# Five changes to a four-layer adjacency kernel: weight sums on VectorE, one eviction split over two engines, an own last turn, statistics ahead, 19 buffers for the residual

## Chip, cores, metric

One core of a Trainium2 chip. The metric is the time of one execution in microseconds (us), lower is better. Times below are medians. A ratio is the mean time of one kernel's fast runs over the mean time of the other's in the same rounds, so it is not quite the ratio of the two medians quoted.

## The reference

x has 128 graphs of 128 nodes with 256 features, float32. Four residual layers follow each other, each behind a layer norm and a relu. The last has two batch norms over all 128 x 128 rows, so nothing after either of them can start before every graph is through.

```python
h = relu(layernorm(x));  x = x + gnn(h, adj)        # layer 0: gates and a 128x128 matrix for each graph
h = relu(layernorm(x));  x = x + attention(h, adj)  # layer 1: causal, added bias
h = relu(layernorm(x));  x = x + slconv3(h, adj)    # layer 2: 256 -> 512 -> 1024 -> 256, mixed by adj*adj
h = relu(layernorm(x))                              # layer 3:
z = A_hat @ h @ W1.T + b1                           #   256 -> 512
o = relu(batchnorm(z)) @ W2.T + b2                  #   512 -> 256
out = x + batchnorm(o)
```

## The kernel before

Four graphs make a group g of T = 512 columns; there are 32 groups. Generators for the layers of several groups are stepped in an order written as a string: FILL for the filling of the pipeline, TURN for each turn after it. A large product is put together from products of quarters of its operands, seven of them in place of eight (`seven`), which needs sums of quarters of each weight (`seven_of`, once) and of each activation (`sums`). Names that begin with p are tiles in PSUM and stand for the products that write them: pc of layer 0, pt, pp and py of layer 1, pu_x near the start of layer 2 and pr at its end, pg and pz of layer 3's first half, po of its second; pm occurs in layers 0 and 2.

```python
    def seven_of(b, name, extra=None):
        ...                                            # four sums for each weight, once
        nc.gpsimd.tensor_tensor(t1, b12, b11, ALU.subtract)
        nc.gpsimd.tensor_tensor(t2, b22, t1, ALU.subtract)
        nc.gpsimd.tensor_tensor(t4n, b21, t2, ALU.subtract)
        nc.gpsimd.tensor_tensor(b12, b22, b12, ALU.subtract)

    def mixed(dst, src, aT, name, evict):
        for c in range(src.shape[-1] // P):
            pm = bank([P, G, P], f"{name}_{c}")
            for b in range(G):
                nc.tensor.matmul(pm[:, b, :], src[:, b, c * P : (c + 1) * P], aT, start=True, stop=True)
            evict(dst[:, c, :], pm.rearrange("p b n -> p (b n)"))
    ...
        h = norm(g, 2)                                 # in layer1(g)
        yield
        mT = w.tile([P, DC, T], FP, tag="dT", name=f"mT_{g}", bufs=2)
        mixed(mT, h, a2T, f"pm2_{g}", nc.scalar.copy)  # "mixed h": pu_x reads mT
    ...
    FILL = "apaapaaaaBBABBBBBBBpBABBBApBABBpABBpABBABB"
    ...
        for k in TURN:
            next(stream[k], None)
    ...
    EARLY, LATE = 4, 11                                # buffers for the residual x3 of the last stage
    ...                                                # pass two: z -> o, group by group; then
    for g in range(EARLY, EARLY + LATE):
        load_later(g)                                  # on GpSimd's queue
    sc2, sh2 = bn_affine(stats2, DC, g2_c, be2_c, "bn2", b2_c)
    ...                                                # scale o, transpose, add x3, store
```

Of the kernel before, what the change touches and what calls it, by code (L numbers as in the profile page):

```python
# [8 lines left out]
FP = mybir.dt.float32  # L9
AF = mybir.ActivationFunctionType  # L10
ALU = mybir.AluOpType
# [4 lines left out]
P = 128  # L16
LN_EPS = 1e-5
BN_EPS = 1e-5
# [4 lines left out]
def kernel(  # L23
# [39 lines left out]
    nc = tc.nc  # L63
    B, N, D = x.shape
    G = 4
    NG = B // G
    T = G * N
    DC = D // P
# [5 lines left out]
    FC = F1 // P  # L74
# [16 lines left out]

    zs = ExitStack()
    zp = zs.enter_context(tc.tile_pool(name="zp", bufs=2, side="right"))
    ZT = {}
# [17 lines left out]
    gw = weights.tile([P, 3, D], FP, name="gw")  # L112
    gb = const.tile([P, 3], FP, name="gb")
    nhalf = const.tile([P, 8], FP, name="nhalf")
    adjT = const.tile([P, P], FP, name="adjT")
    ain = const.tile([P, P], FP, name="ain")
    aout = const.tile([P, P], FP, name="aout")
    maskb = const.tile([P, P], FP, name="maskb")
    a2T = const.tile([P, P], FP, name="a2T")
    ahT = const.tile([P, P], FP, name="ahT")  # L120
    m_qk = weights.tile([P, DC, D], FP, name="m_qk")
# [3 lines left out]
    vecs = const.tile([P, NV], FP, name="vecs")  # L125
    stats1 = const.tile([P, FC, NG, 6], FP, name="stats1")
    stats2 = const.tile([P, DC, NG, 6], FP, name="stats2")
# [50 lines left out]
    for v in (b1, g1, be1, b2, g2, be2):  # L178
        k = v.shape[0] // P
# [18 lines left out]
    def seven_of(b, name, extra=None):  # L198


        b11, b21, b12, b22 = quarters(b)
        if extra is None:
            extra = weights.tile([P, 3, b.shape[1] // 2, b.shape[2] // 2], FP, name=f"{name}_s")
        operands = set_of(b, extra)
        t4n, t1, t2 = operands[3:6]
        nc.gpsimd.tensor_tensor(t1, b12, b11, ALU.subtract)
        nc.gpsimd.tensor_tensor(t2, b22, t1, ALU.subtract)
        nc.gpsimd.tensor_tensor(t4n, b21, t2, ALU.subtract)
        nc.gpsimd.tensor_tensor(b12, b22, b12, ALU.subtract)
        return operands  # L210
# [89 lines left out]
    LAST = NG - 1  # L300
# [25 lines left out]

    def mixed(dst, src, aT, name, evict):

        for c in range(src.shape[-1] // P):
            pm = bank([P, G, P], f"{name}_{c}")  # L330
            for b in range(G):
                nc.tensor.matmul(  # L332
                    pm[:, b, :], src[:, b, c * P : (c + 1) * P], aT, start=True, stop=True
                )
            evict(dst[:, c, :], pm.rearrange("p b n -> p (b n)"))

# [139 lines left out]
    def layer1(g):  # L476
# [83 lines left out]
        mT = w.tile([P, DC, T], FP, tag="dT", name=f"mT_{g}", bufs=2)  # L560
        mixed(mT, h, a2T, f"pm2_{g}", nc.scalar.copy)
        ex = w.tile([P, 3, 1, T // 2], FP, tag="ex", name=f"ms_{g}", bufs=2)
# [16 lines left out]
        uT = w.tile([P, HC1, T], FP, tag="uT", name=f"uT_{g}", bufs=1)  # L579
        mixed(uT, u, a2T, f"pmu_{g}", nc.vector.tensor_copy)  # L580
        ex = w.tile([P, 3, HC1 // 2, T // 2], FP, tag="us", name=f"us_{g}", bufs=1)
# [61 lines left out]
    def layer3(g):  # L643
# [3 lines left out]
        gT = w.tile([P, DC, T], FP, tag="dT", name=f"gT_{g}", bufs=2)  # L647
        mixed(gT, h, ahT, f"pg_{g}", nc.vector.tensor_copy)
        ex = w.tile([P, 3, 1, T // 2], FP, tag="ex", name=f"gs_{g}", bufs=2)
# [19 lines left out]
        yield from seven(columns_by_half(gs, SETS["b"], 0), put, [P, 2, T // 2], f"pz_{g}")  # L669




    TURN = "CCCBCCABBDABBCABBDDCBADCDDBDCCDBACBCCABCCACbBCBBCBCBBCBCBCdB"
    US = {}
    AHEAD = 3
# [5 lines left out]

    FILL = "apaapaaaaBBABBBBBBBpBABBBApBABBpABBpABBABB"
    stream = {"a": layer0(0), "p": prepare(), "B": layer1(0), "A": part(layer0, 1)}
# [5 lines left out]
    for g in range(NG):  # L690
        if g + AHEAD < NG:
            load_x(g + AHEAD)
        stream = {
            "A": part(layer0, g + 2), "B": bs, "C": layer2(g), "D": ds,
            "b": part(layer1, g + 2), "d": layer3(g),
        }
        for k in TURN:
            next(stream[k], None)
        assert all(next(stream[k], k) == k for k in "ABCD")
        bs, ds = stream["b"], stream["d"]  # L700
    for _ in ds:
        pass
    passA.close()

    def bn_affine(stats, nch, gam, bet, name, bias=None):


        mv = const.tile([P, nch, 2], FP, name=f"mv_{name}")
        for j in range(nch):
            nc.vector.bn_aggr(mv[:, j, :], stats[:, j].rearrange("p g s -> p (g s)"))  # L710
        mean = mv[:, :, 0]
        if bias is not None:
            mean = const.tile([P, nch], FP, name=f"mean_{name}")
            nc.vector.tensor_tensor(mean, mv[:, :, 0], bias, ALU.add)
        sc = const.tile([P, nch], FP, name=f"sc_{name}")
        inv_sqrt(sc, mv[:, :, 1], BN_EPS)
        nc.vector.tensor_tensor(sc, sc, gam, ALU.mult)
        sh = const.tile([P, nch], FP, name=f"sh_{name}")
        nc.vector.tensor_tensor(sh, mean, sc, ALU.mult)
        nc.vector.tensor_tensor(sh, bet, sh, ALU.subtract)  # L720
        if bias is not None:
            part = const.tile([P, nch], FP, name=f"part_{name}")
            nc.vector.tensor_tensor(part, bias, sc, ALU.mult)
            nc.vector.tensor_tensor(sh, sh, part, ALU.add)
        return sc, sh
# [4 lines left out]
    O = [keep.tile([P, DC, T], FP, name=f"o_{g}") for g in range(NG)]  # L730
    EARLY, LATE = 4, 11
    x3p = ctx.enter_context(tc.tile_pool(name="x3p", bufs=EARLY, reuse_waits="tile"))
# [3 lines left out]
    zw = zs.enter_context(tc.tile_pool(name="zw", bufs=2, side="right", reuse_waits="tile"))  # L736
    bw2T = keep.tile([P, FC, D], FP, name="bw2T")
    nc.scalar.dma_start(bw2T, BW2T)
    bw2s = keep.tile([P, 3, FC // 2, D // 2], FP, name="bw2s_late")
    nc.scalar.dma_start(bw2s, BW2S)  # L740
# [3 lines left out]
    R = {}  # L744
# [5 lines left out]

    def load_x3(g, pool, tag):
        R[g] = pool.tile([P, G, D], FP, tag=tag, name=f"x3i_{g}")
        nc.gpsimd.dma_start(R[g], X3[g])

    def second(g):
# [28 lines left out]
        def put(ij, pb, other):  # L784
# [7 lines left out]
            if done.count(j) == 2:  # L792
                nc.vector.bn_stats(stats2[:, j, g, :], O[g][:, j, :])

        yield from seven(product, put, [P, T // 2], f"po_{g}", zw)

    for n in range(1, 1 + AT_ONCE):
        load_z(n)
    sc1, sh1 = bn_affine(stats1, FC, g1_c, be1_c, "bn1", b1_c)
    PREPARE = FC + 1  # L800
# [3 lines left out]
    for n, g in enumerate(ORDER):  # L804
        then = second(ORDER[n + 1]) if n + 1 < NG else iter(())
        for _ in range(PREPARE):
            next(now)
            next(then, None)
# [12 lines left out]

    def load_later(g):
        load_x3(g, *((x3p, "x3") if g % (EARLY + LATE) < EARLY else (late, "x3l")))

    for g in range(EARLY, EARLY + LATE):
        load_later(g)
    sc2, sh2 = bn_affine(stats2, DC, g2_c, be2_c, "bn2", b2_c)
    for g in range(NG):
# [54 lines left out]
```

## Time and profile before

| | before |
|---|---|
| median of the three runs known before the prediction | 2664.24 us (2663.99 to 2666.74) |
| TensorE busy | 95% |
| one steady turn (from pr of a group to pr of the next) | 71.65 us |
| TensorE idle in the first 100 us | 50 us |
| gap between the two passes (wait for zo) | 8.0 us |
| from the last product of pass two to the end | 80.8 us |

TensorE is the engine to watch: read this way, a change gains only what it takes from TensorE's idle time, from its slow clock, or from the last stage, where DMA is full. The page's lines are in the prediction below.

### The profile page before, as it was taken

To read this page: it belongs to the slowest core of one execution; us is meant where nothing else is said; L and a number is where in the kernel's file an instruction comes from. 1 tells how busy PE (TensorE), PEld (TensorE's weight loads), DVE (VectorE), ACT (ScalarE), POOL (GpSimd) and SP (SyncE) were. 2 spreads that over 40 slices of the span, in tenths; PEclk is the share of its full clock that TensorE was granted. 3 is DMA by queue.
4 is the path that set the end of the run, shared out by engine and by line. 5 is a ranking of instruction groups with operands and counts; after the bars stand their busy time and mean duration, and the time that the engine had idled before them with its cause. 6 is when DMAs were issued, how large, how long until landed. Compare 5 with 4: busy or idle time off the path is not lost.

```text
span 2665.5 us, 40593 instructions
## 1 busy us (share of the span) xinstructions
PE 2541.2 (95%) x15215; PEld 2283.0 (86%) x15215; DVE 1904.5 (71%) x4743; ACT 1298.8 (49%) x2607; POOL 317.0 (12%) x616
## 2 busy tenths in 40 slices
PE   3899999999999999999999999999999999979984
PEld 2799999989998898999999899988989999968873
DVE  7677777777777777777777777777777776557775
ACT  3454444444455444454444444544454543336655
POOL 4111111111011110111111111111101111000011
PEclk7899999999999999999999999999999999989998
DMA  3000000000000000000000000000000000034469
GB/s 129 15 33 24 25 33 33 33 32 25 25 33 32 32 33 33 33 25 24 32 33 32 32 25 27 29 33 32 32 33 33 28 13 25 32 112 170 171 209 362
DMA packets 62055, 143.05 MB, mean 54 GB/s; under 512 B 4626, under 2 KB 39972, under 8 KB 57892
## 3 DMA queue, kind: packets, MB, share of 16 engines
q1 hardware_dynamic: 51636, 105.60, 11.1%
q0 software_dynamic: 9216, 33.56, 3.2%
q8 instruction: 120, 1.97, 0.3%
q10 hardware_dynamic: 1008, 1.31, 0.2%
q14 instruction: 75, 0.61, 0.1%
HBM read 73.48 MB, written 66.98 MB: 53 GB/s over the span
## 4 chain that ended last, share of the span: by engine, by line
PE 81%; DVE 6%; ACT 4%; DMA 4%; POOL 3%; issue 1%; ACTq 0%; POOLq 0%; DVEq 0%; SPq 0%
PE p_x L377 15%; PE p_z L377 8%; PE p_x L360 7%; PE pu_x L360 4%; PE pmu L332 4%; PE pz_x L377 4%; PE p_y L377 4%; PE po_x L775 3%; PE p_z L360 2%; ACT h L322 2%; PE pg L332 2%; PE pm L469 2%; PE py L551 2%; PE pqv_x L501 2%; PE pqv_x L496 2%; PE ps L521 2%
## 5 line engine op out<-in xcount | busy, mean ns | idle before, releaser
L322 ACT ACTIVATE h<-x,sh,rs 128x256 f32<-128x256 f32 x512 | 268.6, 589 | 386.4 <-POOL sh L319 386.4
L377 PE MATMUL p_x<-uT,w 128*128 128x256 f32 x1024 | 242.1, 379 | 0.0
L608 ACT ACTIVATE h2T<-h2T 128x512 f32<-128x512 f32 x192 | 120.4, 627 | 230.2 <-DVE h2T L607 230.2
L377 PEld LDWEIGHTS p_x<-uT,w 128*128 128x128 f32 x1024 | 189.6, 190 | 23.1
L315 POOL TENSOR_SCALAR rs<-mv 128x4 f32<-128x4 f32 x128 | 29.7, 232 | 1386.9 <-ACT h2T L608 1025.7
L311 DVE BATCH_NORM_STATS2 st<-x 128x6 f32<-128x256 f32 x512 | 190.4, 414 | 4.3 <-DMA x<-in_x_dram 2.1
L429 DVE SCALAR_TENSOR_TENSOR gs<-h,gw 128x256 f32<-128x256 f32 x384 | 163.3, 425 | 34.8 <-ACT h L322 28.8
L392 ACT COPY p_t<-p_x 128x512 f32<-128x512 f32 (+1 forms) x192 | 96.7, 504 | 114.6 <-PE p_x L377 101.9
L316 POOL TENSOR_TENSOR rs<-rs,nhalf 128x4 f32<-128x4 f32 x128 | 147.7, 1154 | 0.0
L332 PEld LDWEIGHTS pmu<-a2T,u 128*128 128x128 f32 x1024 | 119.5, 192 | 17.1 <-PE pr L636 7.4
L360 PEld LDWEIGHTS p_x<-w,h2T 128*128 128x128 f32 x1024 | 124.3, 192 | 3.3
L360 PE MATMUL p_x<-w,h2T 128*128 128x128 f32 x1024 | 124.6, 275 | 0.0
L574 ACT ACTIVATE u<-u 128x512 f32<-128x512 f32 x96 | 60.4, 631 | 131.8 <-DVE u L573 131.8
L764 ACT ACTIVATE zi<-zi,sh_bn,sc_bn 128x512 f32<-128x512 f32 x124 | 97.4, 812 | 55.4 <-DMA zi<-z 35.5
L332 PE MATMUL pmu<-a2T,u 128*128 128x128 f32 x1024 | 119.8, 275 | 1.8 <-ACT u L574 1.8
L377 PE MATMUL p_x<-us,w_s 128*128 128x256 f32 x512 | 121.3, 379 | 0.0
L377 PE MATMUL p_z<-us,w 128*128 128x256 f32 x512 | 121.2, 379 | 0.0
L377 PE MATMUL p_x<-uT,w_s 128*128 128x256 f32 x512 | 121.0, 379 | 0.0
L377 PE MATMUL p_y<-uT,w 128*128 128x256 f32 x512 | 121.0, 379 | 0.0
L377 PE MATMUL p_z<-us,w_s 128*128 128x256 f32 x512 | 121.0, 379 | 0.0
L377 PEld LDWEIGHTS p_z<-us,w 128*128 128x128 f32 x512 | 97.2, 190 | 13.5 <-ACT p_t L392 0.3
L377 PEld LDWEIGHTS p_z<-us,w_s 128*128 128x128 f32 x512 | 97.3, 190 | 13.2
(282 smaller groups left out, 6140.8 us busy)
## 6 DMA issues: line engine op xcount, KB each, us to landing
z<-zo SPq DMA_DIRECT2D x62, 512.0 KB, 2.6
zi<-z SPq DMA_DIRECT2D x31, 1024.0 KB, 4.8
x<-in_x_dram SPq DMA_DIRECT2D x32, 512.0 KB, 3.9
x<-x POOLq DMA_DIRECT2D x32, 512.0 KB, 3.0
x3i<-x POOLq DMA_DIRECT2D x32, 512.0 KB, 6.6
out_dram<-x3i SPq DMA_DIRECT2D x64, 256.0 KB, 8.3
w<-in_L_gnn_W_dram SPq DMA_DIRECT2D x1, 2048.0 KB
w<-in_L_gnn_W_dram SPq DMA_DIRECT2D x1, 1024.0 KB
```

The source lines that it names most:

```text
L311: nc.vector.bn_stats(st[:, b, :], xt[:, b, :])
L316: nc.gpsimd.tensor_tensor(rs, rs, nhalf[:, :G], ALU.pow)
L322: nc.scalar.activation(h[:, b, :], xt[:, b, :], AF.Relu, bias=sh[:, b : b + 1], scale=rs[:, b : b + 1])
L332: nc.tensor.matmul(pm[:, b, :], src[:, b, c * P : (c + 1) * P], aT, start=True, stop=True)
L360: nc.tensor.matmul(pb[:, rr, :], a_r[r][:, c, rr * P : (rr + 1) * P], b_r[r][:, c, :wide], start=(first and rr == 0 and c == 0), stop=(c = ...
L377: nc.tensor.matmul(pb[:, jj, :], b_r[r][:, c, at : at + P], a_r[r][:, c, :], start=(first and jj == 0 and c == 0), stop=(c == nk - 1), ski ...
L392: nc.scalar.copy(t, pb)
L429: nc.vector.scalar_tensor_tensor(gs, h[:, b, :], 1.0, gw[:, i, :], ALU.mult, ALU.mult, accum_out=gl[:, b, i : i + 1],)
L574: nc.scalar.activation(dst, dst, AF.Relu)
L608: nc.scalar.activation(dst, dst, AF.Relu)
L764: nc.scalar.activation(z, z, AF.Relu, bias=sh1[:, j : j + 1], scale=sc1[:, j : j + 1],)
L775: nc.tensor.matmul(pb, BW2R[r][:, c, :], a_r[r][:, c, :], start=(first and c == 0), stop=(c == FC // 2 - 1), skip_group_check=True,)
```

## The change

Its intent: take the port conflict between GpSimd and VectorE out of the filling, take the one wait of a steady turn away, cover the norm of the last group with products of the group before it, take 31 of 32 groups out of the statistics that have to wait for the last one, and load more of the residual ahead.

```diff
     (seven_of)
-        nc.gpsimd.tensor_tensor(t1, b12, b11, ALU.subtract)
+        nc.vector.tensor_tensor(t1, b12, b11, ALU.subtract)
     ... (the three other sums alike)
-            evict(dst[:, c, :], pm.rearrange("p b n -> p (b n)"))
+            evicts[c % len(evicts)](dst[:, c, :], pm.rearrange("p b n -> p (b n)"))
-        mixed(mT, h, a2T, f"pm2_{g}", nc.scalar.copy)
+        mixed(mT, h, a2T, f"pm2_{g}", (nc.vector.tensor_copy, nc.scalar.copy))
+    FINAL = "CCCCCCCCCCCCCCCCCCDCCDCCDdDDdDddDdDdddd"
-    FILL = "apaapaaaaBBABBBBBBBpBABBBApBABBpABBpABBABB"
+    FILL = "paaapaaaAaBBBBBABBBBBBBppABBAApBBABBBpBBAB"
-        for k in TURN:
+        for k in TURN if g < LAST else FINAL:
+    most1 = bn_part(stats1, FC, slice(LAST), "most1")      # 31 groups; joined with the last one later
     ... (bn_affine joins the two parts with six small operations)
-    EARLY, LATE = 4, 11
+    EARLY, LATE = 5, 14
-    bw2T = keep.tile([P, FC, D], FP, name="bw2T")
+    bw2T = second_w.tile([P, FC, D], FP, name="bw2T")      # freed after pass two
     for g in range(EARLY, EARLY + LATE):
-        load_later(g)
+        load_later(g, nc.sync)
     ... (small tiles move to pools that are freed earlier)
```

More of the change, by code (lines that the diff above doesn't have):

```diff
@@ L92 @@
     zs = ExitStack()
+    first = zs.enter_context(tc.tile_pool(name="first", bufs=1, side="right"))
     zp = zs.enter_context(tc.tile_pool(name="zp", bufs=2, side="right"))
@@ L112 @@
     gw = weights.tile([P, 3, D], FP, name="gw")
-    gb = const.tile([P, 3], FP, name="gb")
+    gb = weights.tile([P, 3], FP, name="gb")
     nhalf = const.tile([P, 8], FP, name="nhalf")
-    adjT = const.tile([P, P], FP, name="adjT")
-    ain = const.tile([P, P], FP, name="ain")
-    aout = const.tile([P, P], FP, name="aout")
-    maskb = const.tile([P, P], FP, name="maskb")
-    a2T = const.tile([P, P], FP, name="a2T")
-    ahT = const.tile([P, P], FP, name="ahT")
+    adjT = weights.tile([P, P], FP, name="adjT")
+    ain = weights.tile([P, P], FP, name="ain")
+    aout = weights.tile([P, P], FP, name="aout")
+    maskb = weights.tile([P, P], FP, name="maskb")
+    a2T = weights.tile([P, P], FP, name="a2T")
+    ahT = weights.tile([P, P], FP, name="ahT")
     m_qk = weights.tile([P, DC, D], FP, name="m_qk")
@@ L125 @@
     vecs = const.tile([P, NV], FP, name="vecs")
-    stats1 = const.tile([P, FC, NG, 6], FP, name="stats1")
+    stats1 = first.tile([P, FC, NG, 6], FP, name="stats1")
     stats2 = const.tile([P, DC, NG, 6], FP, name="stats2")
@@ L205, in seven_of @@
         t4n, t1, t2 = operands[3:6]
-        nc.gpsimd.tensor_tensor(t1, b12, b11, ALU.subtract)
-        nc.gpsimd.tensor_tensor(t2, b22, t1, ALU.subtract)
-        nc.gpsimd.tensor_tensor(t4n, b21, t2, ALU.subtract)
-        nc.gpsimd.tensor_tensor(b12, b22, b12, ALU.subtract)
+        nc.vector.tensor_tensor(t1, b12, b11, ALU.subtract)
+        nc.vector.tensor_tensor(t2, b22, t1, ALU.subtract)
+        nc.vector.tensor_tensor(t4n, b21, t2, ALU.subtract)
+        nc.vector.tensor_tensor(b12, b22, b12, ALU.subtract)
         return operands
@@ L325, in norm, with mixed @@
         return h
-    def mixed(dst, src, aT, name, evict):
+    def mixed(dst, src, aT, name, evicts):
         for c in range(src.shape[-1] // P):
@@ L579, in layer1 @@
         uT = w.tile([P, HC1, T], FP, tag="uT", name=f"uT_{g}", bufs=1)
-        mixed(uT, u, a2T, f"pmu_{g}", nc.vector.tensor_copy)
+        mixed(uT, u, a2T, f"pmu_{g}", (nc.vector.tensor_copy,))
         ex = w.tile([P, 3, HC1 // 2, T // 2], FP, tag="us", name=f"us_{g}", bufs=1)
@@ L647, in layer3 @@
         gT = w.tile([P, DC, T], FP, tag="dT", name=f"gT_{g}", bufs=2)
-        mixed(gT, h, ahT, f"pg_{g}", nc.vector.tensor_copy)
+        mixed(gT, h, ahT, f"pg_{g}", (nc.vector.tensor_copy,))
         ex = w.tile([P, 3, 1, T // 2], FP, tag="ex", name=f"gs_{g}", bufs=2)
@@ L669, in layer3, with bn_part @@
         yield from seven(columns_by_half(gs, SETS["b"], 0), put, [P, 2, T // 2], f"pz_{g}")
+    def bn_part(stats, nch, groups, name):
+        mv = const.tile([P, nch, 2], FP, name=f"mv_{name}")
+        for j in range(nch):
+            nc.vector.bn_aggr(mv[:, j, :], stats[:, j, groups].rearrange("p g s -> p (g s)"))
+        return mv[:, :, 0], mv[:, :, 1]
     TURN = "CCCBCCABBDABBCABBDDCBADCDDBDCCDBACBCCABCCACbBCBBCBCBBCBCBCdB"
+    FINAL = "CCCCCCCCCCCCCCCCCCDCCDCCDdDDdDddDdDdddd"
     US = {}
@@ L703, with bn_affine @@
     passA.close()
-    def bn_affine(stats, nch, gam, bet, name, bias=None):
-        mv = const.tile([P, nch, 2], FP, name=f"mv_{name}")
-        for j in range(nch):
-            nc.vector.bn_aggr(mv[:, j, :], stats[:, j].rearrange("p g s -> p (g s)"))
-        mean = mv[:, :, 0]
-        if bias is not None:
-            mean = const.tile([P, nch], FP, name=f"mean_{name}")
-            nc.vector.tensor_tensor(mean, mv[:, :, 0], bias, ALU.add)
+    def bn_affine(most, last, nch, gam, bet, name, bias):
+        (mean, var), (mean1, var1) = most, last
+        share = 1.0 / NG
+        d = const.tile([P, nch], FP, name=f"d_{name}")
+        nc.vector.tensor_tensor(d, mean1, mean, ALU.subtract)
+        nc.vector.scalar_tensor_tensor(mean, d, share, mean, ALU.mult, ALU.add)
+        nc.vector.tensor_tensor(mean, mean, bias, ALU.add)
+        nc.vector.scalar_tensor_tensor(d, d, share * (1.0 - share), d, ALU.mult, ALU.mult)
+        nc.vector.scalar_tensor_tensor(d, var, 1.0 - share, d, ALU.mult, ALU.add)
+        nc.vector.scalar_tensor_tensor(var, var1, share, d, ALU.mult, ALU.add)
         sc = const.tile([P, nch], FP, name=f"sc_{name}")
-        inv_sqrt(sc, mv[:, :, 1], BN_EPS)
+        inv_sqrt(sc, var, BN_EPS)
         nc.vector.tensor_tensor(sc, sc, gam, ALU.mult)
@@ L720, in bn_affine @@
         nc.vector.tensor_tensor(sh, bet, sh, ALU.subtract)
-        if bias is not None:
-            part = const.tile([P, nch], FP, name=f"part_{name}")
-            nc.vector.tensor_tensor(part, bias, sc, ALU.mult)
-            nc.vector.tensor_tensor(sh, sh, part, ALU.add)
+        part = const.tile([P, nch], FP, name=f"part_{name}")
+        nc.vector.tensor_tensor(part, bias, sc, ALU.mult)
+        nc.vector.tensor_tensor(sh, sh, part, ALU.add)
         return sc, sh
@@ L736 @@
     zw = zs.enter_context(tc.tile_pool(name="zw", bufs=2, side="right", reuse_waits="tile"))
-    bw2T = keep.tile([P, FC, D], FP, name="bw2T")
+    second_w = zs.enter_context(
+        tc.tile_pool(name="second_w", bufs=1, side="right", reuse_waits="tile")
+    )
+    bw2T = second_w.tile([P, FC, D], FP, name="bw2T")
     nc.scalar.dma_start(bw2T, BW2T)
-    bw2s = keep.tile([P, 3, FC // 2, D // 2], FP, name="bw2s_late")
+    bw2s = second_w.tile([P, 3, FC // 2, D // 2], FP, name="bw2s_late")
     nc.scalar.dma_start(bw2s, BW2S)
@@ L749, in load_z, with load_x3 @@
         ZT[ORDER[n]] = [z[:, :FC // 2, :], z[:, FC // 2 :, :]]
-    def load_x3(g, pool, tag):
+    def load_x3(g, pool, tag, queue=nc.gpsimd):
         R[g] = pool.tile([P, G, D], FP, tag=tag, name=f"x3i_{g}")
-        nc.gpsimd.dma_start(R[g], X3[g])
+        queue.dma_start(R[g], X3[g])
     def second(g):
@@ L792, in put @@
             if done.count(j) == 2:
-                nc.vector.bn_stats(stats2[:, j, g, :], O[g][:, j, :])
+                nc.vector.bn_stats(stats2[:, j, (g + 1) % NG, :], O[g][:, j, :])
         yield from seven(product, put, [P, T // 2], f"po_{g}", zw)
@@ L798 @@
         load_z(n)
-    sc1, sh1 = bn_affine(stats1, FC, g1_c, be1_c, "bn1", b1_c)
+    last1 = bn_part(stats1, FC, slice(LAST, NG), "last1")
+    sc1, sh1 = bn_affine(most1, last1, FC, g1_c, be1_c, "bn1", b1_c)
     PREPARE = FC + 1
@@ L805 @@
         then = second(ORDER[n + 1]) if n + 1 < NG else iter(())
+        if n + 1 == NG:
+            most2 = bn_part(stats2, DC, slice(LAST), "most2")
         for _ in range(PREPARE):
@@ L820, with load_later @@
     late = ctx.enter_context(tc.tile_pool(name="late", bufs=LATE, reuse_waits="tile"))
-    def load_later(g):
-        load_x3(g, *((x3p, "x3") if g % (EARLY + LATE) < EARLY else (late, "x3l")))
+    def load_later(g, queue=nc.gpsimd):
+        load_x3(g, *((x3p, "x3") if g % (EARLY + LATE) < EARLY else (late, "x3l")), queue)
     for g in range(EARLY, EARLY + LATE):
-        load_later(g)
-    sc2, sh2 = bn_affine(stats2, DC, g2_c, be2_c, "bn2", b2_c)
+        load_later(g, nc.sync)
+    last2 = bn_part(stats2, DC, slice(LAST, NG), "last2")
+    sc2, sh2 = bn_affine(most2, last2, DC, g2_c, be2_c, "bn2", b2_c)
     for g in range(NG):
```

## The prediction

> **What bounds the kernel now.** I read the page's head, then the table of engine time by stretches of the span, then the list of TensorE's waits, then the timeline around each wait. Each `profile` fence copies such lines.
>
> ```profile
> PE 2541.2 (95%) x15215; PEld 2283.0 (86%) x15215; DVE 1904.5 (71%) x4743; ACT 1298.8 (49%) x2607; POOL 317.0 (12%) x616
> ...
> 0.00:20.00 20.00, 6.99 (x29) 5.56 (x29) 10.86 (x44) 7.36 (x15) 7.97 (x21) 1.00 0.89 295
> 20.00:40.00 20.00, 1.87 (x4) 0.72 (x4) 18.96 (x20) 3.35 (x10) 17.74 (x14) 0.53 0.42 135
> 300.00:1300.00 1000.00, 991.38 (x6112) 902.53 (x6110) 731.55 (x1903) 487.53 (x992) 118.42 (x238) 1.00 0.08 30
> 2340.00:2360.00 20.00, 15.12 (x114) 13.41 (x113) 7.10 (x17) 3.04 (x8) 2.31 (x5) 0.98 0.22 79
> 2360.00:2380.00 20.00, 11.36 (x44) 9.13 (x44) 11.84 (x24) 3.98 (x8) 3.31 (x5) 0.76 0.54 203
> 2620.00:2640.00 20.00, 14.49 (x90) 10.49 (x88) 11.44 (x18) 14.72 (x21) 3.69 (x7) 0.91 1.06 396
> ```
>
> The columns of a stretch are its length, the busy time of TensorE, its weight loads, VectorE, ScalarE and GpSimd, then TensorE's clock, the DMA share and GB/s. TensorE bounds all but four places. The first 100 us hold about 50 us of its work. The steady turns leave 0.86% idle. The end of the first pass (2340 to 2380) leaves 13.5 us idle. From about 2576 to the end the DMA engines are full. No change of TensorE's work is in the diff, so the gain can only come out of these places.
>
> ```profile
> PE pu_x L360 <- ACT mT L335: 17.9, 29, 0.6
> PE pc L462 <- DVE m L452: 17.7, 4, 7.3
> PE po_x L775 <- ACT zo L764: 8.0, 1, 8.0
> PE pg L332 <- ACT h L322: 4.4, 1, 4.4
> ...
> 24.21 2.52 POOL L206 TENSOR_TENSOR w_s<-w 128x1024 f32<-128x1024 f32 x1
> 24.45 2.43 DVE L449 SCALAR_TENSOR_TENSOR m<-aout,gt,m 128x128 f32<-128x128 f32 x1
> 1358.61 2.07 ACT L322 ACTIVATE h<-x,sh,rs 128x256 f32<-128x256 f32 x4 [2.74 <-POOL sh L319]
> 1360.59 1.04 ACT L335 COPY mT<-pm 128x512 f32<-128x512 f32 x2
> 1361.21 1.13 PE L360 MATMUL pu_x<-w,mT 128*128 128x256 f32 x4 [0.62 <-ACT mT L335]
> 2359.86 3.78 PE L332 MATMUL pg<-ahT,h 128*128 128x128 f32 x16 [4.41 <-ACT h L322]
> 2575.51 0.54 POOL L753 DMA_DIRECT2D x3i<-x  x1 [195.64 <-PE po_x L775]
> ```
>
> The first four lines are the waits that the change aims at: total us, times, longest. Then the timeline shows a 128x128 VectorE operation of 2.43 us beside a weight sum on GpSimd; the steady wait; the wait at the end of the first pass with the slow matmuls after it; and the first late residual load.
>
> **What the Trainium skill says.** "SBUF — State Buffer", section "SBUF: two separate sides": VectorE with two SBUF inputs and GpSimd hold one port pair by an exclusive lock, and the loser blocks for a whole instruction. The trace agrees: m L449 takes 0.35 us with GpSimd quiet (at 63.43), 2.43 us above. "PSUM — Partial Sum Buffer", section "Specifications (TRN2)": ScalarE and VectorE read PSUM in parallel in different banks. The trace agrees: in the two evictions of hT the ScalarE copy starts at 1385.71 (0.59 us) and VectorE's at 1386.05 (0.69 us), neither stretched. "TensorE: Matmul & The Clock Gate", section "What's actually happening": an idle window of about 3.4 us halves the clock. Agrees: after 4.41 us idle the sixteen pg matmuls take 3.37 us in the chain, against 1.79 in steady turns. "DMA: Bandwidth & Descriptors", section "Issuing engines are not separate DMA queues": all queues run on the same 16 engines, and another queue saves only issue time. I use this for the last part; the before trace alone does not test it.
>
> **Part 1, weight sums on VectorE, new filling order.** Before, gl is ready at 21.7 us, and the twelve VectorE operations that build m run from 22.5 to 39.4, because the sums of w2 and w3 stand between them: a stretch of four GpSimd sums of 2.4 and four of 1.3 us. After, GpSimd is out of the way. VectorE pays for the sums: until gl it has twelve gate products at 0.47 us (the pace at 57 us), eight 128x128 sums at about 0.28, four statistics at 0.35, from 12.96 us: gl near 22.7, 1 us later. Two w1 sums (0.42 each) come next, then m needs about 4.2 us (four of 0.41, eight of 0.32): m is whole at about 28.5 against 39.3. That is 10.7 us. A gate product put between the steps of x gives back about 1 us. The w2 and w3 sums (about 1.2 and 0.7 us each, by the 128x1024 and 128x512 VectorE operations of the trace) stand where VectorE waits for the first norm, or in place of gate products that moved ahead: from hT to p I count 11.8 us against 11.3. **Sum: -9.5 us.**
>
> **Part 2, mixed h on two engines.** The steady wait is ScalarE's: its four h activations end at 1360.7 and only then come both copies. In the built program the first copy stands on VectorE just after s L624, which ends at 1358.86; VectorE is then idle for 2.8 us. So it is done near 1359.6, a microsecond ahead of need. The second stays on ScalarE, 1360.6 to 1361.2; the product that reads it begins after pu_x's 0.86 us, at 1361.5. Both are in time. 29 x 0.62 = 17.9 us; I take 17 for a wait that shows up elsewhere. VectorE gains 0.69 us in a turn of 71.65 us where it is 73% busy. **Sum: -17 us.**
>
> **Part 3, own last turn.** Before, the last group's layer norm leaves TensorE idle for 4.4 us, a residual copy 0.5, smaller waits 1.2, and the slow clock costs about 1.6 (pg) and 1.2 (pz_x 2.08 against 0.86). After, the products of group 30 stand behind the last pr: four and a half of them, 3.9 us of cover. The norm's chain is about 5.5 us now, because a put of group 30 stands in it on VectorE. So about 1.5 us of idle time stays, too short for the clock to fall, and 0.8 for the last put. **Sum: -5 us.**
>
> **Part 4, statistics ahead.** For the first batch norm the aggregation of 31 groups (0.9 us a column) should leave the path. In the built order the four columns are cut in between the last group's own statistics: one stands after the last bn_stats, and two ahead of it in VectorE's queue. Six small dependent operations are added (some 0.2 us each). From gT I count about 14.7 us to the input of pow, against 14.4. **Sum: +0.3 us.** For the second batch norm it is a gain of 0.9 us, and GpSimd's five load issues (2585.23 to 2587.89) no longer delay pow by 0.7 us; but the stores behind it are bound by DMA, so I give it nothing.
>
> **Part 5, 19 buffers and SyncE's queue.** From 2576 to 2664 the DMA engines move 28 loads and 32 groups of stores, 31.5 MB, at 358 GB/s on average. After, one more load (0.52 MB) is early. But in the built program the first late load writes where bw2T lies, so it waits for the last product that reads bw2T (2583.1 in the time of before), and the thirteen others stand behind it in the queue. Before, the first goes out at 2575.5, and by 2583.1 1.9 MB had moved. So 1.4 MB more are left then: 3.7 us at 380 GB/s. Loads that run without the dips of before (290, 292 and 213 GB/s around 2590) give back some 2 us, and the first load's latency takes 1 to 2. **Sum: +3 us.** It is the weakest of the five.
>
> Sum: -9.5 - 17 - 5 + 0.3 + 3 = -28.2; 2664.2 - 28.2 = 2636.0 us.
>
> **Rivals.** (a) *The steady wait only changes its name.* If VectorE's longer list delays puts or sums elsewhere, or ScalarE's second copy comes late, half of part 2 goes: 2645. For it: VectorE is at 73%. Against: the steady turns show no other TensorE wait, and both copies have margins of 1.0 and 0.3 us. (b) *VectorE becomes the bound of the filling*, since 15 us of sums move there and it was 12 to 17 us busy in each 20: part 1 falls to -4, the time is 2641.5. Against: most of its 18.96 us in 20 to 40 was blocked time. (c) *The last stage is a gain after all*: if in-order loads at full rate and free GpSimd count for more than the late start, part 5 is -3 and the time is 2630. (d) *The late loads hurt more*: stores queue behind 7.3 MB of loads on one queue, the recycled loads start late and a stores-only tail at 350 GB/s is left: +7, 2640.
>
> **Range and chances.** (a) and (b) together give about 2650, (c) with a full part 2 and a better last turn about 2626. I take 2626 to 2647. 2% is 53 us, and all idle time of parts 1 to 3 that can go is under 45, so faster by over 2% is 0.03; slower by over 2% would need a new wait in every turn, 0.01.
>
> **What would show it.** Right: pu_x <- mT gone from TensorE's waits and a steady turn of 71.0 instead of 71.65 us; the m operations near 0.35 us and whole by 29 us; the wait of pg under 2 us and its matmuls near 1.8; the wait for zo still 7.5 to 9 us; the first late load some 7 us later, seen from the end of the second pass, with full DMA behind it. Wrong: a new TensorE wait for VectorE (uT, ms or h2s) in each turn, VectorE waits stretching the filling, or a last stage that is shorter than before's 80.9 us from the last po_x (2584.6) to the end.

## The result, and the profile after

| | before | after |
|---|---|---|
| median of 4 runs each, same rounds | 2665.49 us | 2624.99 us (2623.71 to 2625.93) |
| ratio, 95% interval | | 0.9848 (0.9831 to 0.9865) |
| steady turn | 71.65 us | 70.79 us |
| first pr (end of the filling's influence) | 156.44 | 142.59 |

The gain is 40.5 us where 28.2 was predicted; 2624.99 lies just below the range.

The head of the page, the waits of TensorE (total us, times, longest) and three stretches (columns as in the prediction), all of the kernel after:

```profile
PE 2530.3 (97%) x15215; PEld 2275.8 (87%) x15215; DVE 1918.2 (73%) x4819; ACT 1284.4 (49%) x2575; POOL 284.4 (11%) x574
```

```profile
PE po_x L791 <- ACT zo L780: 8.1, 1, 8.1
...
PE pm L333 <- ACT h L323: 6.2, 1, 6.2
...
PE pc L463 <- DVE m L453: 5.5, 3, 4.8
...
PE pg L333 <- ACT h L323: 1.5, 1, 1.5
```

```profile
20.00:40.00 20.00, 7.03 (x19) 4.25 (x20) 15.83 (x53) 7.37 (x18) 5.92 (x9) 0.67 0.42 138
...
2320.00:2340.00 20.00, 10.70 (x38) 8.14 (x37) 15.48 (x40) 8.08 (x14) 3.18 (x5) 0.77 0.89 352
2540.00:2560.00 20.00, 13.32 (x85) 10.80 (x86) 15.27 (x34) 16.18 (x24) 0.72 (x1) 0.83 1.03 401
```

The wait for mT, 29 times in the profile before, is gone. pc waits 5.5 instead of 17.7, pg 1.5 instead of 4.4, and zo the same 8. TensorE does the same 15215 products in 10.9 us less busy time, so part of the gain isn't in the list of waits; section 1 accounts for 29 x 0.24 = 7.0 us of it.

Where the time went can be read off the first product of pr of each group, which exists in both kernels. First before, then after (start, duration):

```profile
156.44 1.88 PE L636 MATMUL pr<-s,a2T 128*128 128x512 f32 x4
228.09 1.88 PE L636 MATMUL pr<-s,a2T 128*128 128x512 f32 x4
```

```profile
142.59 1.88 PE L637 MATMUL pr<-s,a2T 128*128 128x512 f32 x4
213.38 1.88 PE L637 MATMUL pr<-s,a2T 128*128 128x512 f32 x4
```

The filling gave 13.9 us. Each of 29 turns gave 71.65 - 70.79 = 0.86 us, 24.9 in all; at the last pr of group 30 the lead is 38.8 us (2302.91 against 2264.14). From there to the first po_x it is 77.6 us before and 71.5 after, 6.1 us. The last product of pass two ends at 2584.7 and 2539.8, the span at 2665.5 and 2621.9, so the last stage lost 1.3 us (section 7 has all traces). These are two single profiled executions: six other kernels with the old last turn need 76.5 to 77.0 us from that pr to the first po_x, so some 5.2 us are the last turn's and the rest was chance.

Against the prediction's terms: filling -13.9 (said -9.5), steady wait -24.9 (said -17), last turn -5.2 (said -5). Two terms were too small. The experiments ask why.

### The profile page after: what moved, and what is told of

Its sections match the earlier page's. It is cut to its first block, busy times and chain, and to the rows that moved or that the text cites. A ratio compares the mean times of both kernels' runs of the same rounds, so it can differ in the third digit from the quotient of the medians.

```text
span 2621.9 us, 40612 instructions
## 1 busy us (share of the span) xinstructions
PE 2530.3 (97%) x15215; PEld 2275.8 (87%) x15215; DVE 1918.2 (73%) x4819; ACT 1284.4 (49%) x2575; POOL 284.4 (11%) x574
## 4 chain that ended last, share of the span: by engine, by line
PE 90%; DMA 3%; DVE 3%; ACT 2%; issue 1%; POOL 0%; SPq 0%; DVEq 0%; ACTq 0%; POOLq 0%
PE p_x L378 17%; PE p_x L361 9%; PE p_z L378 8%; PE pmu L333 4%; PE p_z L361 4%; PE pu_x L361 4%; PE p_y L378 4%; PE pz_x L378 4%; PE pm L333 2%; PE pg L333 2%; PE ps L522 2%; PE py L552 2%; PE pm L470 2%; PE pqv_x L502 2%; PE p_y L361 2%; PE pqv_x L497 2%
## 5 line engine op out<-in xcount | busy, mean ns | idle before, releaser
L638 DVE TENSOR_TENSOR x<-pr,x 128x512 f32<-128x512 f32 x64 | 43.7, 683 | 90.4 <-PE pr L637 90.4
L378 PEld LDWEIGHTS p_z<-us,w_s 128*128 128x128 f32 x512 | 97.3, 190 | 13.2
```

The source lines that it names most:

```text
L378: nc.tensor.matmul(pb[:, jj, :], b_r[r][:, c, at : at + P], a_r[r][:, c, :], start=(first and jj == 0 and c == 0), stop=(c == nk - 1), ski ...
```

## The experiments

All kernels gave correct results. "Kernel before" in the tables is the kernel before in the same rounds.

### 1. The steady wait alone, and the other way round

```diff
 a1_two_engines, from the kernel before:
-        mixed(mT, h, a2T, f"pm2_{g}", nc.scalar.copy)
+        mixed(mT, h, a2T, f"pm2_{g}", (nc.vector.tensor_copy, nc.scalar.copy))
 a2_second_copy, from the kernel before:
+        mixed(mT, h, a2T, f"pm2_{g}", (nc.scalar.copy, nc.vector.tensor_copy))
```

> The kernel before with one edit: the two copies of mixed h go to VectorE and ScalarE. Theory (a wait of TensorE costs more than its listed idle time, because the product before it runs out and the next one starts up): a steady turn falls from 71.65 to 70.79 us as in the changed kernel, 29 x 0.86 = 25 us in all. Rival (the wait costs what the list shows, 0.62 us, and the rest of the shorter turn comes from another part of the change): a turn of 71.03 us and 18 us in all.

> The kernel before with the two copies of mixed h on two engines the other way round: the first stays on ScalarE, the second goes to VectorE. ScalarE is relieved of just as much work. Theory (only the first copy stands in the path of pu_x): the wait of 0.62 us in each turn stays and the time is the same as before within 1 us. Rival (the gain comes from ScalarE's shorter list): a gain of 10 us or more.

| | median | kernel before | ratio, 95% |
|---|---|---|---|
| a1: first copy on VectorE | 2641.10 | 2664.14 | 0.9911 (0.9896 to 0.9926) |
| a2: second copy on VectorE | 2666.06 | 2664.14 | 1.0003 (0.9991 to 1.0016) |

pr in a1:

```profile
156.47 1.88 PE L636 MATMUL pr<-s,a2T 128*128 128x512 f32 x4
227.26 1.88 PE L636 MATMUL pr<-s,a2T 128*128 128x512 f32 x4
```

The turn is 70.79 us: this one edit makes the whole difference, 23.7 us by the ratio, more than the 17.9 that the list of waits showed for it. The rival, that the rest of the shorter turn comes from another part, is out. a2 relieves ScalarE of just as much work and gains nothing; its list still has the 29 waits of 0.6. Only the copy that pu_x waits for counted.

Where the other 0.24 us of a turn come from is seen in the products around the wait. Before (the line of pu_x at 1361.21 is in the prediction), then after:

```profile
1358.64 1.95 PE L360 MATMUL p_z<-w_s,h2s 128*128 128x128 f32 x16
...
1362.18 1.03 PE L360 MATMUL pu_y<-w,mT 128*128 128x256 f32 x4
```

```profile
1401.79 1.95 PE L361 MATMUL p_z<-w_s,h2s 128*128 128x128 f32 x16
1403.58 1.03 PE L361 MATMUL pu_x<-w,mT 128*128 128x256 f32 x4
1404.44 1.04 PE L361 MATMUL pu_y<-w,mT 128*128 128x256 f32 x4
```

After, pu_x starts 1.79 us after p_z, although p_z lasts 1.95: the last products of one group are still under way when the next begins. Before, it starts 2.57 us after p_z: that is p_z run out to its end (1.95) and the listed 0.62. And pu_y follows 0.97 after pu_x instead of 0.86, because the first product behind the wait starts without its weights loaded ahead: before, its weight load begins together with it (both at 1361.21), after, 0.11 us ahead of it (1403.47 and 1403.58). So the wait costs 0.62 + 0.16 + 0.11 = 0.89 us here (0.16 is 2.57 - 1.79 - 0.62), and 0.86 over a whole turn. "Idle" in the list begins only when the last product has run out. The profile models where a product ends, so how 0.78 divides into 0.62 and 0.16 rests on its model; the 0.78 and the 0.11 are read from starts alone.

### 2. Is that extra a fixed time or a share of the wait?

```diff
 d1_longer_wait, from the kernel before (in layer1, the last h on ScalarE's list before the copies of mixed h):
         h = norm(g, 1)
+        nc.scalar.copy(idle, h[:, G - 1, :4])
```

> The kernel before with a small ScalarE copy (four columns) put just ahead of its two copies of mixed h, so that pu_x waits longer in each turn by what that copy takes. Theory (a wait of TensorE costs its listed idle time plus a fixed 0.24 us of running out and starting up, which is there already): the turn grows by just as much as the listed wait does, the listed wait of 0.62 to about 0.8, the turn from 71.65 to about 71.85 us. Rival (the cost is in proportion to the listed time, 0.86 to 0.62): the turn grows 1.4 times as much as the listed wait.

The time is 2672.31 against 2665.15 us (ratio 1.0028, 1.0012 to 1.0044). TensorE's list of waits in d1, then the second pr (the first is at 156.76):

```profile
PE pu_x L361 <- ACT mT L336: 24.9, 29, 0.9
```

```profile
228.66 1.88 PE L638 MATMUL pr<-s,a2T 128*128 128x512 f32 x4
```

The listed wait grew from 17.9 to 24.9 us, 0.24 for each turn. The turn grew from 71.65 to 71.90, again 0.24. A share of 1.4 would have made it 0.34 and 71.99. So the extra is a fixed 0.24 us for each wait, and removing the wait altogether is worth more than shortening it.

### 3. The filling: sums and order apart and together

```diff
 a3_sums_vector, from the kernel before: the four nc.gpsimd.tensor_tensor of seven_of become nc.vector.tensor_tensor
 a4_new_order, from the kernel before:
-    FILL = "apaapaaaaBBABBBBBBBpBABBBApBABBpABBpABBABB"
+    FILL = "paaapaaaAaBBBBBABBBBBBBppABBAApBBABBBpBBAB"
 b2_sums_and_order: both edits
```

> The kernel before with one edit: the weight sums go from GpSimd to VectorE, in the old filling order. Theory (the shared port is what the filling lost): 9 to 13 us less, m whole before 29 us. Rival (the new order does most of it, and VectorE's longer list eats what the port gives): less than 4 us gained.

> The kernel before with one edit: the new filling order, weight sums still on GpSimd. Theory (the shared port is what the filling lost, the order only fits VectorE's new list): between 3 us less and 3 us more. Rival (the order does most of it): 8 us or more gained.

> The kernel before with the weight sums on VectorE and the new filling order together. The sums alone gave 8.9 us in the trace, the order alone 0. Theory (the order is worth something only once the port is free, because it moves VectorE's longer list to where VectorE waits): the first pr 13.9 us earlier, as in the changed kernel, the time 12 to 14 us less. Rival (the two parts add up, and the other 5 us came from another part, such as where the tiles lie): 8 to 9 us less.

| | median | kernel before | ratio, 95% | m copied from pc at | first pr |
|---|---|---|---|---|---|
| before | | | | 39.32 | 156.44 |
| a3: sums alone | 2656.11 | 2664.14 | 0.9967 (0.9954 to 0.9979) | 28.30 | 147.58 |
| a4: order alone | 2666.09 | 2664.14 | 1.0007 (0.9995 to 1.0020) | 42.58 | 156.47 |
| b2: both | 2651.88 | 2665.78 | 0.9947 (0.9933 to 0.9960) | 26.11 | 144.98 |
| after | 2624.99 | 2665.49 | 0.9848 | 25.79 | 142.59 |

By the ratios the sums alone gain 8.8 us, the order alone nothing that the runs can show, and both 14.1. They don't add up: the order is worth some 5 us, and only once the sums are on VectorE. The intervals of a3 and b2 overlap a little; the traces bear the step out, with the first pr at 147.58 in a3 and at 142.2 to 145.0 in the eight kernels that have both edits. The lists show why. In a3 m is copied 7.1 us after gl, in the kernel after 5.1. ScalarE's gate function comes 1.3 us late in a3, behind a table load (21.40 to 22.68) that is over before gl in the kernel after (whether that is the order's doing isn't shown), and a sum of w2 stands between the operations that build m; the two lines are a3's, the third is the kernel before's, the last two the kernel after's:

```profile
24.14 1.22 DVE L206 TENSOR_TENSOR w_s<-w 128x1024 f32<-128x1024 f32 x1
...
28.30 0.69 DVE L463 COPY m<-pc 128x512 f32<-128x512 f32 x1
```

```profile
39.32 0.68 DVE L463 COPY m<-pc 128x512 f32<-128x512 f32 x1
```

```profile
20.74 0.17 DVE L436 TENSOR_TENSOR gl<-gl,gb 128x12 f32<-128x12 f32 x1
...
25.79 0.69 DVE L464 COPY m<-pc 128x512 f32<-128x512 f32 x1
```

In the new order that sum starts at 34.68, behind the statistics of the next norm. In a4 the same order meets GpSimd's sums at the worst place: gl is ready at 27.51 only, its own operation takes 2.18 us instead of 0.17, and pc waits 19.6 us at a stretch.

One profile each is a small sample. The five kernels with the filling of before have their first pr at 156.1 to 157.0, whether VectorE's first operation on x starts at 7.17 or at 8.35; the eight with both edits (b2, the changed kernel and six built on it) at 142.2 to 145.0. The means are 156.5 and 143.3, so 13.2 us is the better figure for the filling. All of it stands ahead of m: its copy starts at 38.1 to 39.3 in the five and at 25.0 to 26.1 in the eight, and from there to the first pr it takes 117.1 to 118.4 us in the five and 116.8 to 118.9 in the eight.

### 4. How much of the filling is TensorE's clock?

TensorE's clock in the stretches from 20 to 80 us was 0.53, 0.62 and 0.64 before and is 0.67, 0.76 and 0.81 after. Products that nobody reads were put into TensorE's waits, so that it is not idle there.

```diff
 d2_busy_filling, from the changed kernel:
+    def warm(n):
+        pw = bank([P, T], "warm")
+        for _ in range(n):
+            nc.tensor.matmul(pw, ident, gw[:, 0:2, :], start=True, stop=True)
     (for group 0 only: warm(6) ahead of pc, warm(12) ahead of pt, warm(9) ahead of pm2)
 d4_tuned, from c4_three_together (section 7): warm(6), warm(9), warm(9), and warm(5) ahead of pp
```

> The changed kernel with 27 products of 128x512 that nobody reads, put where TensorE waits for group 0 in the filling (ahead of pc, pt and pm2), so that it isn't idle and its clock has no reason to fall. The dependent work is the same. Theory (part of what the filling costs is the slow clock after its waits: granted 0.67, 0.76 and 0.81 in the three stretches from 20 to 80 us): the clock in them near 1.0 and the first pr 3 to 6 us earlier. Rival (the other engines' chain sets the filling, and the slow products are hidden in it): the first pr within 1 us of the changed kernel's.

> The kernel of the three edits with the dummy products cut to fit: nine instead of twelve ahead of pt, where twelve had run 1.2 us past the norm, and five more in the waits for qv and p, after which py still ran at half its pace (3.78 instead of 1.89 us). Theory (the first try gave 2.3 us in the trace rather than 3 to 6 because of these two): pt at 38.4 us or before, py 1.9 us, the first pr near 139 us, the time 2612 to 2613 us. Rival (the chain of the other engines holds the rest): the first pr at 140.5 to 141, the time 2614 to 2615 us.

d2 takes 2621.86 us (ratio 0.9838, 0.9824 to 0.9852), 3 us less than the changed kernel; its first pr is at 140.94. py in d2, and in d4:

```profile
55.63 3.78 PE L562 MATMUL py<-qv,pT 128*128 128x256 f32 x8 [0.78 <-DVE pT L556]
```

```profile
56.41 1.99 PE L564 MATMUL py<-qv,pT 128*128 128x256 f32 x8 [0.78 <-DVE pT L558]
```

In d2 the eight products still run at half pace although the longest wait shortly before them is 2.34 us (for p); filling that wait in part, and an earlier one of 0.88 us, brings them to full pace. Two stretches of d2 (columns as in the prediction) show that the clock fell inside the wait of 2.34 us, which ends at 53.21:

```profile
49.60:52.90 3.30, 1.16 (x8) 0.97 (x8) 3.24 (x10) 3.27 (x8) 0.00 (x0) 1.00 0.00 0
53.00:59.80 6.80, 5.81 (x13) 3.94 (x14) 2.86 (x8) 1.32 (x8) 0.00 (x0) 0.50 0.00 0
```

d2 lies between its theory and its rival. In d4 the clock is 0.91, 1.00 and 1.00 in the stretches from 20 to 80 us, and the first pr is at 139.55, so the clock costs some 143.1 - 139.55 = 3.5 us in the filling of the changed kernel (143.1 is the mean of the changed kernel and the six built on it without dummies). Its time is 2612.79 us, against 2617.42 without the dummies. The clock was a real part of the filling's cost, but at the lower end of the 3 to 6 us expected. What holds the rest of the filling was not taken apart.

### 5. The last turn alone

```diff
 b1_last_turn, from the kernel before:
+    FINAL = "CCCCCCCCCCCCCCCCCCDCCDCCDdDDdDddDdDdddd"
-        for k in TURN:
+        for k in TURN if g < LAST else FINAL:
```

> The kernel before with one edit: its own list of steps for the last turn. Theory (this part was sized right): from the first product of pr of group 30 to the first product po_x 71.5 instead of 76.6 us, the time 5 us less. Rival (this part carries some of what the prediction missed): 9 us or more.

2661.06 against 2665.78 us, ratio 0.9980 (0.9967 to 0.9992): 5.3 us by the ratio, 4.7 by the medians, and the stretch from pr of group 30 to po_x is 71.2 us. The term was sized right. The wait and the products behind it, in the kernel after:

```profile
2316.30 1.20 PE L333 MATMUL pg<-ahT,h 128*128 128x128 f32 x8 [1.45 <-ACT h L323]
```

### 6. Why statistics ahead gain nothing

The prediction gave this part +0.3 us, because four aggregations of 0.98 us stand in VectorE's list beside the last group's own statistics. b4 takes them out of there, by aggregating 30 groups before the last turn. c1 moves the load of the second weights, bw2T, to another queue. c2 does both.

```diff
 b4_earlier_statistics, from the changed kernel:
+        if g == LAST:                                   # ahead of the steps of the last turn
+            most1 = bn_part(stats1, FC, slice(LAST - 1), "most1")
-    most1 = bn_part(stats1, FC, slice(LAST), "most1")   # and the two last groups go into last1
 c1_weights_queue, from the changed kernel:
-    nc.scalar.dma_start(bw2T, BW2T)
+    nc.sync.dma_start(bw2T, BW2T)                       # bw2s alike
 c2_queue_statistics: both edits
```

> The changed kernel with one edit: the part of the first batch norm that is aggregated ahead has 30 groups instead of 31, so that its four operations of 0.98 us stand in the last turn, and not in VectorE's list beside the last group's own statistics. Theory (those operations stand in the path between the two passes): the wait for zo falls from 8.1 to 6 us and the wait for the last put goes, 2 to 3 us less than the changed kernel. Rival (they fill VectorE's idle time there and cost nothing): the same within 1 us, and the wait for zo stays at 8 us.

> The changed kernel with one edit: the loads of bw2T and bw2s go out on SyncE's queue, some 3 us before ScalarE's queue gets to them. Theory (two bounds stand at the same place between the passes: the batch norm's chain and the load of bw2T, which lands some 8 us after its issue): the chain still holds, the same as the changed kernel within 1 us. Rival (the load alone was the bound, and the statistics ahead were a gain already): 2 to 3 us less.

> The changed kernel with both edits: those loads on SyncE's queue, and the statistics of 30 groups aggregated in the last turn. Theory of the two bounds: now both are gone, po_x starts when the first zo activation is done, 2 us after h of the last group rather than 4 us later, and the time is 2 us less than the changed kernel, near 2623 us. Rival (neither stands in the path): the same within 1 us.

| | median (range) | ratio to before |
|---|---|---|
| after | 2624.99 (2623.71 to 2625.93) | 0.9848 |
| b4: 30 groups ahead | 2625.14 (2624.47 to 2626.44) | 0.9847 |
| c1: load on SyncE's queue | 2625.40 (2624.40 to 2626.75) | 0.9847 |
| c2: both | 2622.50 (2622.07 to 2623.05) | 0.9836 |

b4 did not do what its theory said, and the guess that the four operations were harmless was not it either. The issue of bw2T's load, the zo activations and the first product that needs both, in b4 and then in c2:

```profile
2328.99 0.33 ACTq L755 DMA_DIRECT2D bw2T<-BW2T  x1
...
2334.39 2.93 ACT L781 ACTIVATE zo<-zo,sh_bn,sc_bn 128x512 f32<-128x512 f32 x4 [4.82 <-DVE sh_bn L738]
...
2337.41 2.04 PE L792 MATMUL po_x<-zo,bw2T 128*128 128x256 f32 x4 [8.46 <-ACT zo L781]
```

```profile
2325.53 0.32 SPq L755 DMA_DIRECT2D bw2T<-BW2T  x1
...
2334.79 2.08 PE L792 MATMUL po_x<-zo,bw2T 128*128 128x256 f32 x4 [6.31 <-ACT zo L781]
```

In b4 the first zo is ready 0.86 us after 2334.39, but po_x starts 2.2 us later than that, 8.4 us after bw2T's issue. The profile names zo; it is the load. In b1 and in c3 below the profile itself puts this wait down to bw2T; po_x starts 8.2 and 9.2 us after the issue there. In the kernel after both ends meet: po_x starts at 2335.60, 8.1 us after the issue and 0.87 after the zo activations begin. In c2 the load is issued 3.5 us earlier and po_x starts 0.86 us after the zo activations begin (2333.93). So the chain of statistics and the load of bw2T ended at the same time, and either edit alone gains nothing. The ranges of c2 and of the other three do not overlap; the intervals of the ratios alone would not tell them apart.

### 7. The last stage

c3 undoes the last part. b3 keeps it, but gives each late tile its own place, in the order in which the memory comes free, and loads those that lie where the weights were last.

```diff
 c3_last_stage_old, from the changed kernel:
-    EARLY, LATE = 5, 14
+    EARLY, LATE = 4, 11                      # bw2T, bw2s in keep again, load_later(g) on GpSimd's queue
 b3_load_order, from the changed kernel:
-    late = ctx.enter_context(tc.tile_pool(name="late", bufs=LATE, reuse_waits="tile"))
+    late = [... tc.tile_pool(name=f"late{k}", bufs=1, reuse_waits="tile") ... for k in range(LATE)]
+        slot = (13, 12, 11, 10, 9, 8, 7, 6, 5, 1, 0, 4, 3, 2)
     (the three tiles over the last sums and copies are loaded on GpSimd's queue)
 c4_three_together: b3 and both edits of c2;  d3_all_and_busy: c4 and the products of d2
```

> The changed kernel with its last part undone: 4 and 11 buffers, the late loads on GpSimd's queue, bw2T and bw2s in the pool that they had before. Theory (the prediction's: the first load waits for the last product of bw2T, and the part is a loss of 3 us): 2 to 3 us less than the changed kernel. Rival (one more buffer, one queue and a free GpSimd make it a gain): 2 us more or above.

> The changed kernel with one edit: its fourteen late tiles are placed so that the first loads in SyncE's queue write to memory that is free 5 to 18 us before the last product of the second pass, and the tiles that lie where the weights were are loaded last. Theory (the last stage is bound by the DMA engines, and the first load's wait for the last product costs what they could have moved by then): six loads, 3.1 MB, move while the engines are idle, at 400 GB/s 7.9 us less; 5 to 8 us less than the changed kernel, some 2617 to 2620 us. Rival (the last stage is bound by the chain of batch norm, transposes and stores, and the loads are hidden): the same as the changed kernel within 1 us.

> The changed kernel with three edits: late tiles placed so that their loads start early (6.3 us less by itself), loads of the second weights on SyncE's queue, statistics of 30 groups in the last turn. If these add up: 6.3 and 2 us less than the changed kernel, some 2616.5 us, faster than both kernels.

> The kernel of the three edits (late tiles, weights' queue, statistics) with the same 27 products in the filling. If they add up to the 2617.4 us of the three: 2612 to 2614 us by the first theory, 2617 by the rival.

| | median (range) | ratio, 95% |
|---|---|---|
| after | 2624.99 (2623.71 to 2625.93) | 0.9848 (0.9831 to 0.9865) |
| c3: last part undone | 2621.94 (2621.49 to 2623.97) | 0.9836 (0.9822 to 0.9849) |
| b3: places in order of freeing | 2618.76 (2617.86 to 2619.14) | 0.9822 (0.9808 to 0.9835) |
| c4: b3 and c2 | 2617.42 (2616.45 to 2618.40) | 0.9817 (0.9804 to 0.9831) |
| d3: c4 and busy filling | 2614.53 (2612.86 to 2615.37) | 0.9809 (0.9795 to 0.9823) |
| d4: d3 with tuned dummies | 2612.79 (2612.27 to 2614.70) | 0.9806 (0.9793 to 0.9819) |

c3 is some 3 us faster than the changed kernel: the last part is a loss, as large as predicted. The intervals of the two ratios overlap, but three of c3's four runs lie below every run of the changed kernel, and the traces agree: from the last product of pass two to the end it takes 79.2 to 80.8 us in eight of the nine kernels with the old last stage (82.3 in b2, whose profiled run is its slowest), 82.0 to 83.1 in the five with the new one, and 75.9 to 76.3 in the four with b3's places. The first late load and a stretch of the kernel after, and the same stretch of b3:

```profile
2538.16 10.78 SPq L769 DMA_DIRECT2D x3i<-x  x14
```

```profile
2520.00:2540.00 20.00, 19.07 (x85) 15.31 (x83) 15.45 (x28) 9.66 (x21) 0.00 (x0) 1.00 0.18 63
```

```profile
2520.00:2540.00 20.00, 19.34 (x87) 15.63 (x86) 15.86 (x29) 9.66 (x20) 0.11 (x1) 1.00 0.47 159
```

After, the load goes out 0.5 us before the last product po_x (2538.65); before it was 8.1 us (2575.51 against 2583.57). In the 20 us ahead of it the DMA engines move 63 GB/s, since the last z has been loaded and nothing else may start. In b3 they move 159 GB/s there, 1.9 MB more, and the kernel is 6.2 us faster. So the last stage is bound by the DMA engines (busy share 1.03 in the stretch from 2540 shown above), and what counts is when they may begin. b3's gain is a little over the 4.8 us that 1.9 MB take at 400 GB/s; the rest may be the loads on two queues, which no run separates.

c4 is 1.3 us faster than b3 where c2 was 2.5 faster than the changed kernel; the ranges of b3 and c4 overlap, so whether the three edits add up in full isn't shown. d4 is the fastest version, 12.2 us under the changed kernel.

## Why the prediction was wrong

- **Steady wait, the step that failed most.** "29 x 0.62 = 17.9 us; I take 17 for a wait that shows up elsewhere. Sum: -17 us." The mechanism was right: the edit alone removes the wait, nothing took its place, and the swapped copies gain nothing. The size was taken from the list of waits, which shows a wait's idle time only. A wait also lets the product before it run out and makes the next start without its weights: 0.24 us each (turn 0.86 against listed 0.62; same 0.24 when the wait is made longer). 29 x 0.86 = 24.9 us. The discount for a wait elsewhere was wrong too. Together 8 us.
- **Filling.** "Sum: -9.5 us" was 13.2 by the first pr, 14.1 by the ratio. Port, order and the place of the large sums were right; what failed is the length of VectorE's list up to m. From the first gate product (12.96) to "m is whole at about 28.5" it allowed 15.5 us; the eight kernels with both edits take 12.5 to 13.9. Gate products with a sum between them follow each other after 0.34 + 0.21 us (the step of such a pair in the trace after), not after 0.47 + 0.28, and its own terms add up only to 22.2 for gl and, from "gl near 22.7", to 27.7 for m: 0.5 and 0.8 us of it have no term. So m gains 13.1 us (the means of the two sets) and not 10.7. It then took some 1.2 us off for what lies behind m ("gives back about 1 us", "11.8 us against 11.3"), and that stretch is as long as before (117.9 and 117.8 us on average). The clock, which it left out here, shows no part in the gain: over the 60 us from m's copy on it is 0.72 before and 0.76 after. It costs 3.5 us in the changed filling all the same. Together 4 us.
- **Last turn.** "Sum: -5 us": 5.3 alone by the ratio. "About 1.5 us of idle time stays" and "0.8 for the last put": 1.45 and 1.16. Right in the sum, and near in both parts.
- **Statistics ahead.** "From gT I count about 14.7 us to the input of pow, against 14.4": 14.2 after and 14.5 before. The verdict, nothing gained, was right, but its reason only half: the load of bw2T ends at the same time and would have held po_x anyway.
- **Last stage.** "Sum: +3 us", called the weakest: c3 says 3, with an uncertainty as large, and the traces' last stages say about 2. The first load is 7.6 us later against the end of pass two, "some 7" had been said.
- **Rivals.** (a) and (b), which made the gain smaller, did not occur; (c), a last stage that gains, did not either. The case that came, the two large terms both too small, was not among them: all waits were taken at their listed length, and the range was cut off at 2626 for that reason.

The parts measured one by one, by the ratios, give -23.7 - 14.1 - 5.3 + 3.2 = -39.9 us against -40.5 for the whole, so little is left for the statistics. Each of these has some 4 us of uncertainty, so that they meet this closely is in part luck.

## What to carry to other kernels

A wait of the busiest engine can cost more than its listed idle time; here TensorE paid 0.24 us more for running out and starting up, whatever the wait's length (0.62 and 0.86). Size its removal by the distance between two products in a stretch with the wait and in one without it. When an operation moves to another engine, the order of that engine's list has to move with it: here each edit alone was worth 9 and 0 us, both together 14. And where a gap has two ends that fall together, a chain of small operations and a transfer issued late, neither edit alone shows anything; try them together before calling either useless.

## What the Trainium skill lacked or had wrong

- "TensorE: Matmul & The Clock Gate", sections "Single matmul latency" and "LDWEIGHTS (loading the stationary operand)", has both parts of what a wait costs beyond its idle time, but does not put them together for a wait in a stream: a constant of about 166 ns of a product that nothing overlaps, and 128 / 1.2 ns, an estimate of 107 ns, for a load of weights. Here they are 0.16 and 0.11 us around one wait, and 0.24 us for each wait over whole turns, the same at listed waits of 0.62 and 0.86 us. The runs agree with the load of weights and with the sum; the 0.16 alone is no independent test, since the profile models the ends of products. The prediction had not used it.
- The same page, section "HAM oscillation — how this bites in real kernels", warns of idle gaps over about 3.4 us. Here a shorter one was enough: in d2 the granted clock fell from 1.00 to 0.50 inside a wait of 2.34 us, with TensorE busy for 1.16 of the 3.30 us before the fall, and the eight products py behind it took 3.78 instead of 1.99 us. With that wait cut to 1.05 us and an earlier one of 0.88 us filled, in d4, the clock stayed at 1.00; which of the two was needed isn't separated. A single gap of 1.45 us did not do it (eight pg products in 1.20 us).
